# A convolutional attention block on one core: the work beside the attention steps ordered by a small planner

## The chip, the core and the metric

The kernel runs on one core of a Trainium2 chip. Its engines are TensorE (PE, matmul, with PEld as its weight loads), VectorE (DVE), ScalarE (ACT), GpSimd (POOL) and SyncE (SP, which here issues DMAs). Each engine runs its own queue in order; a semaphore holds back an instruction whose data or buffer isn't ready, and with it everything behind it on that engine. The metric is the device time of one execution in microseconds (us).

## The reference

The input x has 8 images of 64 x 64 positions with 256 channels (4096 positions an image), all in float32. Two layers follow each other. Cut to what matters:

```python
# layer 0
q, k = jnp.split(x @ w_qkv + b_qkv, 2, axis=-1);  v = k
ctx_h = _sdpa(h_windows(q), h_windows(k), h_windows(v))   # channels 0..127: 8 windows of 8 rows, 4 heads of 32
ctx_v = _sdpa(v_windows(q), v_windows(k), v_windows(v))   # channels 128..255: 8 windows of 8 columns, 4 heads of 32
hv = hard_swish(v)
bias_branch = depthwise_conv_3x3(hv, dw) + dw_bias
context = hard_swish(concat(ctx_h, ctx_v) + bias_branch)
x = context @ w_out + b_out
# layer 1: spectrally normed weights kf, kg, kh (256 to 32) and kv (32 to 256)
f, g, h = x @ kf + bf, x @ kg + bg, x @ kh + bh
beta = softmax(g @ f.T)                                    # 4096 x 4096 for each image
out = gamma * ((beta @ h) @ kv + bv) + x
```

## The kernel before

Channels lie on partitions, positions along the free axis, in 8 blocks of 512 positions. For each image there are 8 horizontal window units (h0 to h7), 8 vertical ones (v0 to v7) and 8 global ones (l0 to l7, each 512 queries against all 4096 positions). A window unit has 4 steps, a global one 8, so an image has 128 steps and the kernel 1024. The units run in the order h, v, h0 of the next image, l, then h1 and so on.

A step scores(c) is four matmuls (one for each group of 32 partitions) into one set of four PSUM banks (the pool ps_sc has one buffer) and one exponential on ACT over 128 x 2048 values (L281) into a weight buffer p. There are three weight buffers (pool ptp). One step later, weighted(c) multiplies the weights with the values (L467 for windows, L622 for global units) into num. The function run_units walks through all steps: scores of this step, pieces that must come first, the weighted product of the step before, then the pieces that were put at this step.

The sums of the weights, which the softmax divides by, are made in part on DVE and in part on PE. In a window unit, weights 0 and 1 are added on DVE into acc (L476, at step 2, when weighted(1) runs); the sum of acc over keys is a product with ones on PE at step 3, and weights 2 and 3 are summed by two products (L480) at step 0 of the next unit. In a global unit each step adds its weights into acc on DVE (L628, L630); at the end acc is folded (L636, L637) and summed by one product. acc has one buffer for all units. release copies num to SBUF on ACT (L489, L634). norm (L288 to L292 and L494 or L643) transposes the sums, takes their reciprocals, transposes back and multiplies; for vertical units it then sends the result through DRAM (via, shuf) to get back to the row layout (L501, L503 on SP).

The other pieces are:

- project(i, m, k): half a projection of block i, a product of four 512-column matmuls (L68); with k = 1 also the evacuation on ACT (L343 to L362). m = 0 and 2 are queries and keys of the horizontal windows, m = 1 and 3 those of the vertical windows.
- values(kind, i): 16 small matmuls that transpose the keys of a block (pv, L68) and a copy on ACT (L425).
- swish(i, half): hard swish of the keys on DVE (L374, L386) into hv, with halo rows copied by POOL (L393, L394).
- conv(i, half, taps): the depthwise convolution of a block and half of the channels into act. Tap 0 is an activation on ACT (L402), taps 1 to 8 are each one DVE instruction (L406).
- context of a unit: adds the attention to act and applies the hard swish (L517 or L524, L526, L527 on DVE).
- next_layer(i): the projection for layer 1 (pf), an evacuation on ACT (L543), five DMAs on SP, and a transposition of h (ph, L553, L558).
- queries of a global unit: four DMAs on SP (L574); result(m, k): thirds of the output projection (po), an evacuation (L664) and a DMA (L665).

The order of the pieces is written out by hand at the end of attention: spread deals a list of pieces evenly over given steps, finish_window puts release at step 0 and norm at step 1 of the next unit, ahead of what is there, finish_global places norm and the six thirds of the output at fixed steps. Convolutions run in four pieces of two DVE taps (the first with tap 0), one in each step of a unit. A second, exact path repeats the computation where a check of the sums fails; it isn't taken with these inputs.

Of the kernel before, what the change touches and what calls it, by code (L numbers as in the profile page):

```python
# [2 lines left out]

# [12 lines left out]
P = 128  # L16
# [16 lines left out]
class Unit:  # L33
# [4 lines left out]
    def __init__(self, steps, scores, values):  # L38
        self.steps, self.scores, self.values = steps, scores, values
        self.at = [[] for _ in range(steps)]  # L40
        self.first = [[] for _ in range(steps)]


def run_units(units):
    held = None

    def late():
        nonlocal held
        if held is not None:
            held[0].values(held[1])  # L50
        held = None

    for unit in units:
        for c in range(unit.steps):
            unit.scores(c)
            for piece in unit.first[c]:
                piece()
            late()
            for piece in unit.at[c]:
                piece()  # L60
            held = (unit, c)
    late()
# [9 lines left out]
def tile_attention_blocks(  # L72
# [181 lines left out]
    def attention(images, load_x, out_rows, exact):  # L254
# [3 lines left out]
        sfx = "e" if exact else ""  # L258
        state = pools.enter_context(tc.tile_pool(name=f"state{sfx}", bufs=1))
# [5 lines left out]
        ptp = pools.enter_context(tc.tile_pool(name=f"ptp{sfx}", bufs=2 if exact else 3))  # L265
# [32 lines left out]
        def negated_rows(negm, name):  # L298
# [12 lines left out]
            nm = work.tile([P, TB], F32, tag="nm", name=f"nm_{name}", bufs=2)  # L311
# [5 lines left out]
        def image(b):  # L317
            hv, qh, kh, kn, xt, vs, part = {}, {}, {}, {}, {}, {}, {}
            recs = work.tile([P, 3 * NB, TB // D], F32, tag="recs", name=f"recs_{b}")

            def note():
                for t, op in zip(seen, (ALU.max, ALU.min)):
                    nc.vector.tensor_tensor(t, t, recs, op)

# [83 lines left out]
            def conv_pieces(i, half):  # L408
                return [
                    lambda t=t: conv(i, half, t) for t in ((0, 1, 2), (3, 4), (5, 6), (7, 8))  # L410
                ]

# [14 lines left out]
            def window_unit(kind, i):  # L427
# [34 lines left out]
                def weighted(c):  # L462
                    if c == 0:
                        u["num"] = ps_av.tile([P, TB], F32, tag="num", name=f"num_{nm}")
                        u["sum"] = ps_av.tile([P, TB], F32, tag="sum", name=f"sum_{nm}")
# [6 lines left out]
                    if c == 1:  # L472
                        u["acc"] = work.tile(
                            [P, NQ, TB], F32, tag="acc", name=f"acc_{nm}", bufs=1
                        )
                        nc.vector.tensor_add(u["acc"], u.pop(0), u.pop(1))  # L476
# [401 lines left out]
```

## Time and profile before

| what | value |
|---|---|
| timed runs | 4035.29, 4036.5, 4038.03 us; median 4036.5 us |
| profiled execution | 4039.26 us, of it span from first to last instruction 4037.4 us |
| mean granted TensorE clock | 0.980 |
| POOL busy | 163.0 us (4%) |
| x loads on SP | 113 of 512 KB, 3.9 us each from issue to landing |
| chain that ended last | PE 57%, ACT 24%, DVE 12%, issue 3%, DMA 2% |
| costliest group | L281 ACT, global exponentials: 512 x 1.880 us = 962.5 us |
| taps on DVE (L406) | 1024 x 0.749 us = 766.0 us |
| adds of weights on DVE | 384 x 2.292 us (L630), 64 x 2.292 (L628), 2 x 64 x 2.285 (L476) |

A row such as "L476 DVE TENSOR_TENSOR acc_v<-p_v,p_v" names the source line, the engine, the operation and the tiles that are written and read. In the timeline, the first two numbers are start and duration in us; the bracket at the end is the engine's idle time just before, and what ended it. Busy shares are means over stages in which different things are waited for, so that what a piece costs is read from the steps around it.

### The profile page before, as it was taken

Reading aid. Unit: us, or ns where it says so; the run is one execution under the profiler, and the core shown is the slowest. Engines: PE = TensorE matmul, PEld = TensorE weight load, DVE = VectorE, ACT = ScalarE, POOL = GpSimd, SP = SyncE. Lnnn points to the kernel's source line nnn. Section 1 sums busy time; section 2 is a strip of 40 time slices with the busy share of each in tenths; the row PEclk is TensorE's granted clock in tenths of the full one; section 3 lists DMA queues with packets and bytes.
Section 4 is the critical chain, followed back from the end, with each engine's and each line's share of the span. In section 5 each row is a group of like instructions: output and inputs, shape, how many; then the busy total and the mean of one; then the engine's idle time right before and its main releaser. Section 6 shows DMA issues by size and latency. Waiting matters only on the chain.

```text
span 4037.4 us, 74304 instructions
## 1 busy us (share of the span) xinstructions
PE 3638.5 (90%) x32296; PEld 1030.2 (26%) x32296; DVE 2992.6 (74%) x3308; ACT 2530.1 (63%) x2058; POOL 163.0 (4%) x521
## 2 busy tenths in 40 slices
PE   7988998889988899898998899988999889998887
PEld 2222222222222222222222222222222222222221
DVE  4776778767787677876778767787677867777776
ACT  4655766656666666666666666665676656666565
POOL 0000000000000000000000001000010000000000
PEclk9999999999999999999999999999999999999999
DMA  1011110111101111011110111101111011110100
GB/s 39 17 38 43 50 51 17 44 45 44 53 12 44 46 53 43 14 47 43 51 48 12 50 49 43 49 13 52 41 50 43 13 50 44 48 43 19 43 27 30
DMA packets 126335, 157.64 MB, mean 39 GB/s; under 512 B 20528, under 2 KB 62000, under 8 KB 126000
## 3 DMA queue, kind: packets, MB, share of 16 engines
q1 hardware_dynamic: 123312, 152.12, 12.2%
q8 instruction: 255, 4.18, 0.4%
q10 hardware_dynamic: 2688, 0.69, 0.1%
q14 instruction: 80, 0.66, 0.1%
HBM read 77.23 MB, written 50.33 MB: 32 GB/s over the span
## 4 chain that ended last, share of the span: by engine, by line
PE 57%; ACT 24%; DVE 12%; issue 3%; DMA 2%; SPq 1%; ACTq 0%; DVEq 0%
ACT p_l L281 15%; PE s_l L604 15%; PE pq L68 8%; PE s_h L450 7%; ACT p_h L281 5%; PE num_l L622 4%; DVE act L406 4%; PE po_l L68 4%; PE num_h L467 3%; PE sum_h L480 3%; PE s_v L450 3%; PE pv L68 3%; PE sum_v L480 3%; DVE acc_v L476 2%; ACT p_v L281 2%
## 5 line engine op out<-in xcount | busy, mean ns | idle before, releaser
L281 ACT ACTIVATE p_l<-s_l 128x2048 f32<-128x2048 f32 x512 | 962.5, 1880 | 535.7 <-PE s_l L604 503.0
L406 DVE SCALAR_TENSOR_TENSOR act<-hv,dw_sb,act 128x512 f32<-128x512 f32 x1024 | 766.0, 749 | 374.4 <-ACT act L402 350.9
L630 DVE TENSOR_TENSOR acc_l<-acc_l,p_l 128x2048 f32<-128x2048 f32 x384 | 880.1, 2292 | 50.9 <-ACT p_l L281 27.2
L604 PE MATMUL s_l<-g_l,f 32*128 32x512 f32 x4096 | 609.2, 648 | 124.2 <-ACT p_l L281 69.9
L281 ACT ACTIVATE p_v<-s_v 128x2048 f32<-128x2048 f32 x256 | 481.2, 1880 | 354.5 <-DVE acc_v L476 185.4
L281 ACT ACTIVATE p_h<-s_h 128x2048 f32<-128x2048 f32 x256 | 481.4, 1881 | 206.0 <-PE s_h L450 186.8
L622 PE MATMUL num_l<-p_l,h_sb 128*32 128x512 f32 x4096 | 546.3, 605 | 0.1
L68 PE MATMUL pq<-x,wqkv_sb 128*32 128x512 f32 x4096 | 521.0, 601 | 24.4 <-DMA x<-in_xT 15.5
L628 DVE TENSOR_TENSOR acc_l<-p_l,p_l 128x2048 f32<-128x2048 f32 x64 | 146.7, 2292 | 319.7 <-ACT p_l L281 319.7
L450 PE MATMUL s_v<-qv,kv 32*128 32x512 f32 x2048 | 295.9, 648 | 80.7 <-ACT p_v L281 79.3
L450 PE MATMUL s_h<-qh,kh 32*128 32x512 f32 x2048 | 296.6, 649 | 39.7 <-ACT p_h L281 39.7
L604 PEld LDWEIGHTS s_l<-g_l,f 32*128 32x128 f32 x4096 | 173.7, 185 | 582.1 <-ACT p_l L281 485.1
L467 PE MATMUL num_h<-p_h,vs 128*32 128x512 f32 x2048 | 278.8, 617 | 0.0
L467 PE MATMUL num_v<-p_v,vs 128*32 128x512 f32 x2048 | 273.6, 606 | 0.0
L68 PE MATMUL po_l<-act,wout_sb 128*32 128x512 f32 x2048 | 253.9, 593 | 0.0
L393 POOL COPY hv<-hv 128x64 f32<-128x64 f32 x112 | 124.5, 1112 | 3100.6 <-DVE hv L386 3100.6
L68 PEld LDWEIGHTS pq<-x,wqkv_sb 128*32 128x32 f32 x4096 | 134.1, 111 | 336.6 <-issue 303.1
L622 PEld LDWEIGHTS num_l<-p_l,h_sb 128*32 128x32 f32 x4096 | 80.5, 108 | 382.7 <-issue 333.5
L476 DVE TENSOR_TENSOR acc_h<-p_h,p_h 128x2048 f32<-128x2048 f32 x64 | 146.3, 2286 | 10.8 <-ACT p_h L281 10.7
L480 PE MATMUL sum_v<-acc_v,ones 128*32 128x512 f32 x512 | 74.8, 659 | 87.8 <-DVE acc_v L476 87.8
L450 PEld LDWEIGHTS s_v<-qv,kv 32*128 32x128 f32 x2048 | 81.6, 186 | 264.2 <-ACT p_v L281 200.0
L476 DVE TENSOR_TENSOR acc_v<-p_v,p_v 128x2048 f32<-128x2048 f32 x64 | 146.2, 2284 | 0.0
(192 smaller groups left out, 3095.0 us busy)
## 6 DMA issues: line engine op xcount, KB each, us to landing
x<-in_xT SPq DMA_DIRECT2D x113, 512.0 KB, 3.9
out<-ot_l SPq DMA_DIRECT2D x128, 256.0 KB, 2.0
via_v<-nums_v SPq DMA_DIRECT2D x64, 256.0 KB, 2.0
shuf_v<-via_v SPq DMA_DIRECT2D x256, 64.0 KB, 2.0
g_l<-gq SPq DMA_DIRECT2D x256, 64.0 KB, 2.0
f<-fgh SPq DMA_DIRECT2D x256, 16.0 KB, 1.8
gq<-fgh SPq DMA_DIRECT2D x64, 64.0 KB, 2.0
wqkv_sb<-in_w_qkv SPq DMA_DIRECT2D x1, 512.0 KB, 3.8
```

The source lines that it names most:

```text
L68: nc.tensor.matmul(out[quad(r), :], lhsT=lhsT[:, quad(r)], rhs=rhs, start=start, stop=stop)
L281: nc.scalar.activation(pt, sc, AF.Exp, scale=scale)
L393: nc.gpsimd.tensor_copy(before[:, 9, 1 : W + 1], v[:, 1, 1 : W + 1])
L406: nc.vector.scalar_tensor_tensor(o, src, wt, o, ALU.mult, ALU.add)
L450: nc.tensor.matmul(sc[:, r, :], lhsT=k[quad(r), c * P : (c + 1) * P], rhs=q[quad(r), :], start=True, stop=not exact,)
L467: nc.tensor.matmul(u["num"][quad(r), :], lhsT=vs[kind, i][:, c, quad(r)], rhs=u[c][:, r, :], start=(c == 0), stop=(c == 3),)
L476: nc.vector.tensor_add(u["acc"], u.pop(0), u.pop(1))
L480: nc.tensor.matmul(u["sum"][quad(r), :], lhsT=ones[:, :D], rhs=pt[:, r, :], start=(z == "acc"), stop=(z == 3),)
L604: nc.tensor.matmul(sc[:, r, :], lhsT=f4[quad(r), c, :], rhs=u["g"][quad(r), :], start=True, stop=not exact,)
L622: nc.tensor.matmul(u["num"][quad(r), :], lhsT=h_sb[:, c * 4 + r, :], rhs=pt[:, r, :], start=(c == 0), stop=(c == NB - 1),)
L628: nc.vector.tensor_add(u["acc"], u.pop(0), u.pop(1))
L630: nc.vector.tensor_add(u["acc"], u["acc"], u.pop(c))
```

## The change

Nothing that is computed changes; the order in which pieces are put into the engines' queues does. The classes Unit and run_units, and the hand-written places, are taken out. A planner (Flow) walks through the same 1024 steps in the same order. A Task has pieces, a cost, a due step, other tasks that it needs (with a lag in steps) and an earliest step. Two lanes are kept: lane 0 for PE work, lane 1 for DVE work. In each step the fixed pieces of that step come first; then each lane takes the waiting task that is due first, until its budget of 3.25 or 3.3 is used. Costs are constants in the source. What is needed and hasn't been placed is called up at once by require.

The sums of a window unit move: the add of weights 0 and 1 stays at step 2, as a fixed piece; the sum of acc is at step 3, that of weights 2 at step 0 of the next unit, that of weights 3 at its step 1, and norm is at its step 2. In a global unit the sum product stays two steps after the unit's end and norm moves to three steps after it. The projection for layer 1 is split in two pieces. A load of x is issued when the last piece that reads its buffer has been placed, and its own readers wait two steps. The core of the diff, in the lines of the changed kernel:

```diff
-class Unit:
-def run_units(units):
+PROD, ADD, FOLD, NORM, SWISH, TAPS, CONTEXT = 0.86, 2.3, 1.95, 2.5, 1.15, 1.5, 1.9
+class Flow:
+    def require(self, *tasks):
+        for task in tasks:
+            if task.done is not None:
+                continue
+            if task.blockers:
+                self.require(*task.blockers)
+            elif task in self.waiting[0] + self.waiting[1]:
+                self.require(*(n for n, _ in task.needs))
+                while task.done is None:
+                    self.piece(task)
+    def choose(self, lane):
+        if lane == 0 and self.open is not None:
+            return self.open
+        tasks = [k for k in self.waiting[lane] if k.can_start(self.t)]
+        return min(tasks, key=lambda k: k.due) if tasks else None
+    def step(self, scores, values):
+        spent = list(self.base) if scores else [0.0, 0.0]
+        spent[1] += self.behind
+        if scores:
+            scores()
+        for piece in self.first.pop(self.t, ()):
+            piece()
+        if self.held:
+            self.held()
+        self.held = values
+        for piece, lane, cost in self.fixed.pop(self.t, ()):
+            piece()
+            spent[lane] += cost
+        for lane in range(2):
+            goal = self.fill[lane]
+            if lane == 0:
+                goal = max(goal + self.spare, spent[lane] + self.rate())
+            while True:
+                task = self.choose(lane)
+                if task is None or spent[lane] + task.cost / 2 > goal:
+                    break
...
+                spent[lane] += task.cost
+                self.piece(task)
+        self.spare = min(max(self.spare + self.fill[0] - spent[0], -PROD / 2), PROD / 2)
+        self.behind = max(0.0, spent[1] - self.fill[1])
+        self.t += 1
...
-                    if c == 1:
-                        u["acc"] = work.tile(
...
-                        nc.vector.tensor_add(u["acc"], u.pop(0), u.pop(1))
-                    for z in {2: ["acc"], 3: [2, 3]}.get(c, ()):
...
+                def add():
+                    u["acc"] = work.tile([P, NQ, TB], F32, tag="acc", name=f"acc_{nm}", bufs=1)
+                    nc.vector.tensor_add(u["acc"], u.pop(0), u.pop(1))
+                def sums(z):
...
+        flow = Flow(base=(1.95, 0.0), fill=(3.25, 3.3))
...
+        for u in units:
+            e = u.t + u.steps
+            if hasattr(u, "fold"):
+                for c in range(1, NB):
+                    flow.at(u.t + c + 1, partial(u.add, c), 1, ADD)
+                u.released = fixed_piece(e, partial(lambda u: (u.must(), u.release()), u))
+                flow.at(e, u.fold, 1, FOLD)
+                flow.at(e + 2, u.sums, 0, PROD)
+                u.normed = fixed_piece(e + 3, u.norm, 1, NORM)
+            elif hasattr(u, "add"):
+                flow.at(u.t + 2, u.add, 1, ADD)
+                for c, z in ((3, "acc"), (4, 2), (5, 3)):
+                    flow.at(u.t + c, partial(u.sums, z), 0, PROD)
+                u.released = fixed_piece(e, partial(lambda u: (u.must(), u.release()), u))
+                u.normed = fixed_piece(
+                    e + 2, partial(lambda u: (u.must_norm(), u.norm()), u), 1, NORM
+                )
...
+            def conv_task(i, half):
+                needs = [(sw[min(i + 1, NB - 1), half], 2)]
+                if last:
+                    needs += [(k, 0) for k in last.results[i]]
+                due = (h[i].t + 7) if half == 0 else v[i].t + 7
+                taps = ((0, 1, 2), (3, 4), (5, 6), (7, 8))
+                pieces = [partial(im.conv, i, half, k) for k in taps]
+                cv[i, half] = flow.add(1, Task(pieces, TAPS, due, needs))
...
+                    lag = 3 if kind else 1
+                    context[kind, i] = flow.add(
+                        1,
+                        Task(
+                            [u.context], CONTEXT, u.t + (11 if kind else 9),
+                            [(cv[i, kind], 0), (u.normed, lag)],
+                        ),
+                    )
...
+                if i > 1:
+                    h[i].must = lambda i=i, context=context: flow.require(context[0, i - 2])
+                    v[i].must_norm = lambda i=i, context=context: flow.require(context[1, i - 2])
+                    l[i].must = lambda i=i, im=im: flow.require(*im.results[i - 2])
...
-        def spread(unit, pieces, steps):
-        def finish_window(unit, after):
-            after.at[0].insert(0, unit.release)
-            after.at[1].insert(0, unit.norm)
-        def finish_global(unit, after):
...
         with tc.manual_schedule():
-            start()
-            run_units(units)
-            end(units[-1])
+            order_loads()
+            for u in units:
+                for c in range(u.steps):
+                    assert flow.t == u.t + c
+                    flow.step(partial(unit_scores, u, c), partial(unit_values, u, c))
+            flow.drain()
```

The rest of the diff builds the tasks of projections, transpositions, swishes, results and loads in the same way.

## The prediction

> **What bounds the kernel now.** I read the engines' shares first, then the table of waits, then the timeline of two units, then the granted clock in short windows.
>
> ```profile
> PE 3638.5 (90%) x32296; PEld 1030.2 (26%) x32296; DVE 2992.6 (74%) x3308; ACT 2530.1 (63%) x2058; POOL 163.0 (4%) x521
> ```
>
> No engine is full over 4037.4 us, so order decides. The 1024 attention steps follow one another through one set of score banks: scores (PE), exponential (ACT), and only then the next scores. Everything else of a step is queued in between. The timeline of ACT gives the price of a step, from one exponential (L281) to the next.
>
> ```profile
> 1653.66 1.88 ACT L281 ACTIVATE p_h<-s_h 128x2048 f32<-128x2048 f32 x1 [0.54 <-PE s_h L450]
> ...
> 1659.16 1.88 ACT L281 ACTIVATE p_h<-s_h 128x2048 f32<-128x2048 f32 x1 [0.44 <-PE s_h L450]
> ...
> 1720.97 1.88 ACT L281 ACTIVATE p_v<-s_v 128x2048 f32<-128x2048 f32 x1 [0.55 <-PE s_v L450]
> 1722.74 0.58 ACT L489 COPY nums_v<-num_v 128x512 f32<-128x512 f32 x1
> 1723.21 0.82 ACT L402 ACTIVATE act<-hv,dwb_sb,dw_sb 128x512 f32<-128x512 f32 x1
> 1724.75 1.88 ACT L281 ACTIVATE p_v<-s_v 128x2048 f32<-128x2048 f32 x1 [0.72 <-PE s_v L450]
> 1727.95 1.88 ACT L281 ACTIVATE p_v<-s_v 128x2048 f32<-128x2048 f32 x1 [1.32 <-PE s_v L450]
> 1730.59 0.69 ACT L543 ACTIVATE fgh<-pf,bcomb 96x512 f32<-96x512 f32 x1 [0.76 <-PE pf L68]
> 1733.53 1.88 ACT L281 ACTIVATE p_v<-s_v 128x2048 f32<-128x2048 f32 x1 [2.25 <-DVE acc_v L476]
> ```
>
> Call a group of four 512-column matmuls beside the attention (half a projection, a sum of weights, a third of an output) one product; a block's transposition counts as one. The first pair, a step with four products, is 5.50 us. In the unit from 1720.97 the step with two products takes 3.78, the one with none 3.20. So a product costs 0.86 above two, and a step costs 3.20 with up to one, 3.78 with two, 4.64 with three, 5.50 with four. The last step there has two (3.78) and took 5.58: its exponential waited for the add of weights, DVE L476. DVE in the same unit:
>
> ```profile
> 1724.07 1.54 DVE L406 SCALAR_TENSOR_TENSOR act<-hv,dw_sb,act 128x512 f32<-128x512 f32 x2 [3.36 <-ACT act L402]
> 1725.52 0.69 DVE L517 TENSOR_TENSOR tmp_v<-shuf_v,act 128x512 f32<-128x512 f32 x1
> ...
> 1727.31 0.71 DVE L288 STREAM_TRANSPOSE zt_v<-sum_v 128x512 f32<-128x512 f32 x1
> ...
> 1729.70 1.53 DVE L406 SCALAR_TENSOR_TENSOR act<-hv,dw_sb,act 128x512 f32<-128x512 f32 x2
> 1731.15 2.28 DVE L476 TENSOR_TENSOR acc_v<-p_v,p_v 128x2048 f32<-128x2048 f32 x1
> ```
>
> Read it as a queue. The taps start at 1724.07, 3.10 after the unit's first exponential, because tap 0 stands on ACT behind the exponential and the evacuation. Then two taps (0.75 each), a context (start to next start 1.79), the norm (1727.31 to 1729.70: 2.39), two taps, the add; 0.10 after its end the fourth exponential starts. It needs the buffer of weights 0, which the add frees (three buffers). The waits say how much this is:
>
> ```profile
> ACT p_v L281 <- DVE acc_v L476: 185.4, 57, 9.7
> ACT p_h L281 <- DVE acc_h L476: 15.3, 8, 1.9
> DVE act L406 <- ACT act L402: 350.9, 120, 5.7
> ```
>
> **What the old order costs.** The steps of the old order by products: 493 with none or one, 432 with two, 29 with three, 56 with four, 13 with five, one with eight: 1577.6+1633.0+134.6+308.0+82.7+8.9 = 3744.7 us. The first exponential starts at 46.9. So 4037.4-46.9-3744.7 = 245.8 us are lateness beyond these prices: per image 8.4 where the first vertical unit's fourth exponential waits 9.7, some 5.6 and 4.0 around the two borders to and from the global units, 1.65 net in each of five vertical units; the rest is small or the last step's.
>
> **The change, part by part.** Work is conserved: the same matmuls, activations and vector instructions; only seven more loads of x on SP (120 for 113).
>
> *Evener steps.* The new order has 472 steps with none or one, 454 with two, 77 with three, 11 with four, 8 with five, one with seven, one with eight: 1510.4+1716.1+357.3+60.5+50.9+17.0 = 3712.2. Gain 32.5 us. It is no more because below two products a step can't go under 3.20. Ahead of the first exponential stand four products instead of nine: -5 x 0.86 = -4.3.
>
> *Old lateness.* The piles behind it (eight taps, two contexts and a norm ahead of the add in the first vertical unit; queries just ahead of the first global unit) are dissolved. All 245.8 goes out of the sum, and I count the new lateness from nothing, in a steady image.
>
> *The norm moves to the add's step.* With weights 2 and 3 summed in the next unit's steps 0 and 1, the norm goes from step 1 to step 2, fixed pieces in order of units: on DVE it stands directly ahead of the pair's add, which still must end before the fourth exponential. The planner also puts a whole half of a convolution (eight taps) into steps 0 and 1, where before two taps stood in each step. So, from the first exponential:
> - v1: 3.10 + 8 x 0.75 + 2.39 + 2.28 + 0.10 = 13.87; its three steps have 1, 2, 0 products: 3.20+3.78+3.20 = 10.18. Late 3.7.
> - v2, v3: 3.10 + 6 x 0.75 + 1.79 + 2.39 + 2.28 + 0.10 = 14.16 against 1, 2, 2 products, 10.76. Late 3.4 each. v4 to v7 have no taps left: nothing.
> - h3: in step 1 tap 0 stands on ACT behind a query evacuation; 3.8 late, h4 2.3, h5 2.5; each gives back some 0.6, as the following step's PE work is done by then. Net 3.3+1.6+2.0.
> - h0: norm and add behind a copy of h: 1.3.
>
> *A new wait on ACT.* The copy that evacuates a unit's numerators (L489) reuses the buffer of the unit two before, whose context must be done. Where the planner is behind, that context is called up in the same step, behind a half of taps: h6 and v0. In v0: tap 0 ends 2.6 after the exponential before, + 8 x 0.75 + 0.73 (the context's first add) = 9.3; then copy and tap 0 (1.3 net), and behind them on ACT the next exponential: 10.6 against 6.4. Late 4.2. Then 0.15 + 6.0 + 2.39 + 2.28 + 0.10 = 10.9 to the fourth, against 3.78+3.20: 3.9 more. h6 likewise: 4.4 and 3.1, 0.6 back. Together 8.1+6.9.
>
> *Global units.* acc has one buffer, so a unit's first add waits for the sum product of the unit before, in step 2. It starts 1.7 after that step's exponential: 1.7+2.29+0.10 = 4.1 against 3.20, four units x 0.9. In units 3 and 5, keys and a tap 0 lie together on ACT (0.69+0.68+0.82) and four taps ahead of the add in one: 1.6 and 3.1. Unit 7: 0.4. Together 8.7. Bounds for these: nothing (the adds lag within three buffers) and twice.
>
> Sum per image: v1 to v3 10.5, v0 8.1, h6 6.9, h3 to h5 6.9, h0 1.3, global 8.7: 42.4. Eight images: 339.
>
> *Moved DMAs.* The norm's write and four reads, and the loads of x, move on SP; a row of context waits for shuf only 0.7 us in all today, and lag three steps (over 9.6 us) is kept for them. The seven loads take 3.9 each to land and are issued two steps ahead, so 0; without that cover 27 us.
>
> *Clock.* Two windows of the profile: columns are length, busy time of PE, PEld, DVE, ACT, POOL, then the granted clock.
>
> ```profile
> 1566.00:1569.40 3.40, 1.17 (x16) 0.48 (x16) 2.63 (x4) 2.30 (x3) 0.00 (x0) 1.00 0.41 146
> 1569.50:1572.90 3.40, 3.40 (x16) 0.52 (x8) 0.37 (x1) 0.69 (x1) 0.00 (x0) 0.50 0.00 0
> ```
>
> After a stretch with 1.17 us of PE work in 3.40, the next ran at half clock. The late units leave PE idle for 2.1 to 4.5 us, eleven times an image. A sum product at half clock (1.7) still fits under an exponential (1.88); sum and transposition (1.8 to 3.6) don't: 1.7 in each of h3 to h6, say 6 an image, 48 in all. Bounds: 0, and 1.9 in each of eleven, 21 an image. [...]
>
> Last step's lateness as now 13.9; transposition steps 3.86 for 3.78, 16 x 8 x 0.08 = 10.
>
> 4037.4 - 4.3 - 32.5 - 245.8 + 339 + 48 + 13.9 + 10 = 4165.7. The profiled run's own time is 4039.26 and the runs shown lie 0.9 us below the span; I forecast **4165**.
>
> **Rivals.**
> - *Taps not held by tap 0* (faster). If DVE had its taps ready at a unit's start, 3.10 would go in v1 to v3, v0, h6 and about as much again over h3 to h5: 21 an image, and most of the idle gaps: 4165-170-40 = 3955. It decides once new lateness, clock included, is under 32 an image instead of 48. For it: planner lags between swish and convolution. Against: the 350.9 us that DVE waits for tap 0 in 120 cases today. 0.06.
> - *The order isn't what the fill aims at, old lateness stays*: 4037.4-36.8 = 4000. Against: the counts of steps did change. 0.02.
> - *Evacuation copies do not wait* (the contexts come in time): without 4.2 and 4.4, 4100. Against: eight taps can't be done in one step. 0.13.
> - *The clock drops at each gap*: 4165+120 = 4285. For: today each idle stretch over 2.2 us shows it. 0.13.
> - My sum: 0.66.
>
> **Numbers.** The range 4095 to 4260 holds the likeliest case, the case without ACT's wait and part of the clock's. No change that a measurement can tell means within 0.2%, 8 us. Faster 0.08 (first two), same 0.01, slower 0.91.
>
> **What would show it.** Waits of p_v and p_h for the pair's add grow from 200 us to over 250 and spread to the horizontal units; the 9.7 us wait goes; nums copies show waits for DVE; steps with two products stay 3.78; more short stretches at 0.50 clock. Wrong if the fourth exponentials wait under 1 us each, or if the global units change by more than 100 us either way.

## The result and the profile after

The changed kernel takes 4244.39 us (median; 4237.78 to 4245.94), the kernel before 4036.22 in the same comparison. The ratio is 1.0512, with a 95% interval of 1.0494 to 1.053: slower by about 5%, as forecast, and inside the range, but 79 us above the 4165 forecast. The profiled execution took 4237.78 us, its span 4235.9, its mean granted clock was 0.961 (0.980 before).

First the engines' shares of the changed kernel:

```profile
PE 3711.2 (88%) x32296; PEld 1036.5 (24%) x32296; DVE 3020.8 (71%) x3308; ACT 2521.8 (60%) x2058; POOL 112.2 (3%) x521
```

The instruction counts of PE, PEld, DVE, ACT and POOL are those of before: no work was added. PE was busy 73 us longer with the same matmuls, so some ran slower; for the other 126 of the 198 us it stood idle longer. The table of waits (who waits, for whom: us in all, times, longest) says where:

```profile
DVE act L496 <- ACT act L492: 500.7, 127, 10.1
...
ACT p_v L369 <- DVE acc_v L559: 144.1, 36, 5.7
ACT p_h L369 <- DVE acc_h L559: 142.3, 42, 5.3
ACT p_l L369 <- DVE acc_l L719: 130.3, 56, 3.7
DVE acc_l L719 <- PE sum_l L155: 121.9, 28, 6.4
...
ACT nums_h L575 <- DVE tmp_h L610: 75.5, 15, 5.4
```

(L369 is the exponential, L559 and L719 the adds, L492 and L496 the taps, L155 the products, L575 the evacuation.) Before, exponentials of windows waited 185.4 + 15.3 = 200.7 us for the add, nearly all in vertical units, up to 9.7 each. Now it is 286.4, spread evenly over both kinds. Two more stand out: exponentials of global units wait for their first add (130.3, 32.7 before), which itself now waits for the sum product of the unit before, and the evacuation of horizontal units waits for a context, a wait that wasn't there before.

One unit shows the first of these. DVE in v1 of the fourth image (start, us, engine, line, operation, out<-in; the bracket is idle time and who ended it):

```profile
1817.13 6.26 DVE L496 SCALAR_TENSOR_TENSOR act<-hv,dw_sb,act 128x512 f32<-128x512 f32 x8 [5.55 <-ACT act L492]
1823.32 0.71 DVE L376 STREAM_TRANSPOSE zt_v<-sum_v 128x512 f32<-128x512 f32 x1
...
1825.09 0.69 DVE L580 TENSOR_TENSOR nums_v<-nums_v,rr_v 128x512 f32<-128x512 f32 x1
1825.70 2.28 DVE L559 TENSOR_TENSOR acc_v<-p_v,p_v 128x2048 f32<-128x2048 f32 x1
```

and ACT there:

```profile
1814.04 1.88 ACT L369 ACTIVATE p_v<-s_v 128x2048 f32<-128x2048 f32 x1 [2.27 <-PE s_v L535]
...
1821.20 1.88 ACT L369 ACTIVATE p_v<-s_v 128x2048 f32<-128x2048 f32 x1 [0.54 <-PE s_v L535]
1828.08 1.88 ACT L369 ACTIVATE p_v<-s_v 128x2048 f32<-128x2048 f32 x1 [4.99 <-DVE acc_v L559]
```

Eight taps, which began 3.09 us after the unit's first exponential, then the norm, then the add: the fourth exponential starts 14.04 after the first (the prediction added up 13.87), against 10.18 by the prices.

The second, ACT at the start of v0 of the same image:

```profile
1790.99 1.88 ACT L369 ACTIVATE p_v<-s_v 128x2048 f32<-128x2048 f32 x1 [0.62 <-PE s_v L535]
1797.55 0.58 ACT L575 COPY nums_h<-num_h 128x512 f32<-128x512 f32 x1 [4.68 <-DVE tmp_h L610]
1798.03 0.81 ACT L492 ACTIVATE act<-hv,dwb_sb,dw_sb 128x512 f32<-128x512 f32 x1
1798.74 1.87 ACT L369 ACTIVATE p_v<-s_v 128x2048 f32<-128x2048 f32 x1
```

The copy waits 4.68 us, and the next exponential is behind it in ACT's queue, though its scores were long done on PE:

```profile
1792.92 1.14 PE L535 MATMUL s_v<-qv,kv 32*128 32x512 f32 x8 [0.21 <-ACT p_v L369]
```

The third is in the global units. The first add of l1 of the same image, the fourth and fifth exponentials, and the scores between them:

```profile
1977.66 2.29 DVE L719 TENSOR_TENSOR acc_l<-p_l,p_l 128x2048 f32<-128x2048 f32 x1 [6.42 <-PE sum_l L155]
1980.04 1.88 ACT L369 ACTIVATE p_l<-s_l 128x2048 f32<-128x2048 f32 x1 [2.33 <-DVE acc_l L719]
1981.97 2.07 PE L694 MATMUL s_l<-g_l,f 32*128 32x512 f32 x8 [2.07 <-ACT p_l L369]
1984.15 1.88 ACT L369 ACTIVATE p_l<-s_l 128x2048 f32<-128x2048 f32 x1 [2.23 <-PE s_l L694]
```

PE is idle for 2.07 us until that exponential is done, and the next scores take 2.07 us, where the eight of v0 above took 1.14. Windows around this (length, busy time of PE, PEld, DVE, ACT, POOL with counts, then granted clock, DMA share, GB/s):

```profile
1975.20:1978.60 3.40, 3.17 (x32) 0.73 (x24) 0.94 (x1) 2.51 (x3) 0.00 (x0) 1.00 0.81 225
1978.60:1982.00 3.40, 1.33 (x16) 0.19 (x12) 3.30 (x6) 1.88 (x1) 0.50 (x4) 1.00 0.03 6
1982.00:1985.40 3.40, 3.40 (x16) 0.86 (x20) 3.37 (x3) 1.25 (x1) 0.00 (x0) 0.51 0.01 2
```

In the second window the exponential of the fourth step waits for the first add, so PE has only 1.33 us of work; in the third the clock is 0.51, and 16 of PE's instructions take longer than 32 did in the first. Summed over the trace's clock records, PE stood at half clock for 330.9 us in 77 stretches, against 162.6 in 26 before.

By the terms of the prediction (first exponential, steps at their prices, lateness beyond them): 46.9 + 3744.7 + 245.8 before, 42.7 + 3712.2 + 481.0 now. The steps did become cheaper, as counted; the lateness, forecast at 411 with clock and last step, came to 481. By kind of unit, horizontal units went from 1108.7 to 1182.3 us in all, vertical ones from 1077.5 to 1083.1, global ones from 1804.3 to 1927.8: more than half of the loss lies in the global units.

### The profile page after: what moved, and what is told of

It is laid out like the page before. It is cut to its first block, busy times and chain, and to the rows that moved or that the text cites. A ratio compares the mean times of both kernels' runs of the same rounds, so it can differ in the third digit from the quotient of the medians.

```text
span 4235.9 us, 74363 instructions
## 1 busy us (share of the span) xinstructions
PE 3711.2 (88%) x32296; PEld 1036.5 (24%) x32296; DVE 3020.8 (71%) x3308; ACT 2521.8 (60%) x2058; POOL 112.2 (3%) x521
## 4 chain that ended last, share of the span: by engine, by line
PE 54%; DVE 24%; ACT 18%; issue 3%; DMA 0%; ACTq 0%; DVEq 0%; POOL 0%; POOLq 0%
PE s_l L694 12%; DVE act L496 11%; ACT p_l L369 9%; PE pq L155 7%; PE num_l L710 7%; PE po_l L155 6%; PE s_v L535 4%; PE s_h L535 4%; ACT p_v L369 3%; DVE acc_l L719 3%; PE sum_h L566 3%; PE num_v L551 3%; PE num_h L551 2%; ACT p_h L369 2%; DVE acc_h L559 2%
## 5 line engine op out<-in xcount | busy, mean ns | idle before, releaser
L369 ACT ACTIVATE p_l<-s_l 128x2048 f32<-128x2048 f32 x512 | 962.2, 1879 | 624.2 <-PE s_l L694 477.3
L496 DVE SCALAR_TENSOR_TENSOR act<-hv,dw_sb,act 128x512 f32<-128x512 f32 x1024 | 769.3, 751 | 533.1 <-ACT act L492 500.7
L369 ACT ACTIVATE p_v<-s_v 128x2048 f32<-128x2048 f32 x256 | 480.8, 1878 | 337.3 <-PE s_v L535 191.0
L369 ACT ACTIVATE p_h<-s_h 128x2048 f32<-128x2048 f32 x256 | 480.8, 1878 | 275.8 <-DVE acc_h L559 142.3
L710 PE MATMUL num_l<-p_l,h_sb 128*32 128x512 f32 x4096 | 570.0, 630 | 0.1
L155 PE MATMUL pq<-x,wqkv_sb 128*32 128x512 f32 x4096 | 501.2, 599 | 0.1
L535 PE MATMUL s_v<-qv,kv 32*128 32x512 f32 x2048 | 308.3, 673 | 55.0 <-ACT p_v L369 52.8
L551 PE MATMUL num_v<-p_v,vs 128*32 128x512 f32 x2048 | 289.7, 640 | 30.4 <-ACT nums_h L575 28.8
L155 PE MATMUL po_l<-act,wout_sb 128*32 128x512 f32 x2048 | 270.1, 622 | 0.0
L719 DVE TENSOR_TENSOR acc_l<-p_l,p_l 128x2048 f32<-128x2048 f32 x64 | 146.5, 2290 | 172.5 <-PE sum_l L155 121.9
L155 PEld LDWEIGHTS pq<-x,wqkv_sb 128*32 128x32 f32 x4096 | 135.1, 112 | 315.5 <-issue 313.3
L483 POOL COPY hv<-hv 128x64 f32<-128x64 f32 x112 | 66.5, 594 | 3215.2 <-DVE hv L476 3171.5
L559 DVE TENSOR_TENSOR acc_h<-p_h,p_h 128x2048 f32<-128x2048 f32 x64 | 146.3, 2286 | 7.1 <-PE sum_l L155 5.9
L566 PE MATMUL sum_h<-p_h,ones 128*32 128x512 f32 x1024 | 147.0, 648 | 0.0
L559 DVE TENSOR_TENSOR acc_v<-p_v,p_v 128x2048 f32<-128x2048 f32 x64 | 146.2, 2285 | 0.0
```

The costliest lines, as they stand in the source:

```text
L155: nc.tensor.matmul(out[quad(r), :], lhsT=lhsT[:, quad(r)], rhs=rhs, start=start, stop=stop)
L369: nc.scalar.activation(pt, sc, AF.Exp, scale=scale)
L483: nc.gpsimd.tensor_copy(before[:, 9, 1 : W + 1], v[:, 1, 1 : W + 1])
L496: nc.vector.scalar_tensor_tensor(o, src, wt, o, ALU.mult, ALU.add)
L535: nc.tensor.matmul(sc[:, r, :], lhsT=k[quad(r), c * P : (c + 1) * P], rhs=q[quad(r), :], start=True, stop=not exact,)
L551: nc.tensor.matmul(u["num"][quad(r), :], lhsT=vs[kind, i][:, c, quad(r)], rhs=u[c][:, r, :], start=(c == 0), stop=(c == 3),)
```

## The experiments

All times are medians of the comparison. The kernel before was run beside each and took 4031 to 4036 us; ratios are to it, with 95% intervals. Lateness and half-clock time are worked out from each kernel's own trace as above.

| kernel | us | ratio | steps at their prices | lateness | half clock, us (stretches) |
|---|---|---|---|---|---|
| before | 4036.2 | 1 | 3744.7 | 245.8 | 162.6 (26) |
| changed | 4244.4 | 1.0512 (1.0494 to 1.053) | 3712.2 | 481.0 | 330.9 (77) |
| add_first | 4066.8 | 1.0072 (1.0055 to 1.0089) | 3712.2 | 319.0 | 225.0 (53) |
| sums_back | 4040.3 | 1.0012 (0.9999 to 1.0025) | 3717.7 | 273.5 | 218.2 (47) |
| ctxh3 | 4288.5 | 1.0621 (1.0603 to 1.0638) | 3720.5 | 523.5 | 416.1 (91) |
| after_t | 4148.7 | 1.0281 (1.0264 to 1.0299) | 3717.1 | 390.0 | 303.7 (70) |
| lsum1 | 4124.1 | 1.0232 (1.0215 to 1.0249) | 3706.2 | 373.8 | 249.5 (46) |
| warm8 | 4221.1 | 1.046 (1.0442 to 1.0477) | 3712.2 without the added | | 252.9 (52) |
| warml6 | 4234.3 | 1.0496 (1.0479 to 1.0514) | 3712.2 without the added | 482.7 | 286.3 (57) |
| bsums | 4039.4 | 1.0023 (1.0014 to 1.0033) | 3688.7 | 297.6 | 165.4 (19) |
| bbest | 3964.7 | 0.9834 (0.9818 to 0.9851) | 3744.7 | 171.7 | 133.1 (13) |
| sb_l1 | 3922.5 | 0.9727 (0.9711 to 0.9744) | 3711.7 | 167.3 | 75.1 (14) |
| best_fill325 | 3867.1 | 0.9582 (0.9566 to 0.9598) | 3716.0 | 108.5 | 82.3 (11) |
| best | 3798.0 | 0.9412 (0.9396 to 0.9428) | 3693.8 | 63.1 | 38.3 (6) |

### The norm behind the add (add_first)

```diff
         for u in units:
+            if hasattr(u, "add") and not hasattr(u, "fold"):
+                flow.at(u.t + 2, u.add, 1, ADD)
+        for u in units:
             e = u.t + u.steps
...
-                flow.at(u.t + 2, u.add, 1, ADD)
```

The order that the planner fills does not change otherwise; only two neighbours in DVE's queue change places.

> The changed kernel with one edit: in the third step of a window unit the add of weights 0 and 1 is queued on DVE ahead of the norm of the unit before, not behind it; everything else keeps its place. Theory (the norm's 2.39 us ahead of the add is what the fourth exponential waits for): v0 to v3, h3 to h6 and h0 give back up to 2.39 us each, some 19 us an image, 150 us over eight images, and up to 30 more because fewer idle stretches slow the clock: 4060 to 4100 us, and the waits of p_v and p_h for the add fall from 286 us to about 130. Rival (the late norm then holds up the sum product that needs its bank, and the contexts behind it): less than 60 us come back, 4185 us or more, with new waits of PE for DVE's transposition. Second rival (the clock is the main cost): under 30 us come back.

4066.8 us: 178 came back, as expected. DVE in the same unit, v1 of the fourth image:

```profile
1734.82 4.69 DVE L496 SCALAR_TENSOR_TENSOR act<-hv,dw_sb,act 128x512 f32<-128x512 f32 x6
1739.43 2.28 DVE L559 TENSOR_TENSOR acc_v<-p_v,p_v 128x2048 f32<-128x2048 f32 x1
1741.63 0.71 DVE L376 STREAM_TRANSPOSE zt_v<-sum_v 128x512 f32<-128x512 f32 x1
```

and the waits:

```profile
DVE tmp_v L603 <- DMA shuf_v<-via_v: 187.7, 42, 7.1
...
ACT p_v L369 <- DVE acc_v L559: 66.3, 31, 3.9
PEld sum_v L566 <- DVE zt_v L376: 50.4, 28, 3.2
ACT p_h L369 <- DVE acc_h L559: 42.6, 25, 3.0
PEld sum_h L566 <- DVE zt_h L376: 42.5, 28, 3.0
```

The exponentials' wait for the add falls from 286.4 to 108.9 us. The two traced runs differ by 165 us (one was the longest of its four, the other the shortest); by their steps the window units are 172 shorter and the global ones some 10 longer. The rival's waits are there too: PE for the late norm's transposition, and contexts for their loads (73.3 us in the changed kernel). They cost little here: a sum product and a context had slack, the add had none.

### The sums and the norm as before (sums_back)

```diff
-                for c, z in ((3, "acc"), (4, 2), (5, 3)):
+                for c, z in ((3, "acc"), (4, 2), (4, 3)):
...
-                    e + 2, partial(lambda u: (u.must_norm(), u.norm()), u), 1, NORM
+                    e + 1, partial(lambda u: (u.must_norm(), u.norm()), u), 1, NORM
```

> The changed kernel with one part undone: the sum products of weights 2 and 3 go together into the next unit's first step, and the norm into its second, as before the change; the planner fills around them. Theory (norm and eight taps together ahead of the add make the fourth exponential late): with the norm a step earlier the planner puts only two taps beside it and the rest behind the add, so v2, v3 and h5 lose their 3.4, 3.4 and 2.6 us, v1 goes from 3.9 to some 2.2, v0 and h6 have three taps fewer ahead of the waiting copy (2.2 each): about 20 us an image, 4055 to 4090 us. Rival (the planner's piling of taps is enough by itself, wherever the norm stands): within 50 us of the changed kernel, 4195 or more.

4040.3 us, 15 less than the lower end of what was expected, and not to be told from the kernel before. With the norm in the second step the planner places two taps beside it and the others behind the add; v2, v3 and h5 are then on time, the fourth exponential of v1 is 2.2 late instead of 3.8, and the first steps of h6 and v0 0.2 and 0.8 instead of 4.6. h0, h6 and v0 are still 7.3, 2.1 and 4.5 late over their four steps. So the loss is the pair: the norm at the add's step, and a planner that fills the two steps before it with eight taps.

### Three buffers for the copies (ctxh3)

```diff
                     u["num_sb"] = work.tile(
-                        [P, TB], F32, tag="nums" if kind else "ctxh", name=f"nums_{nm}"
+                        [P, TB], F32, tag="nums" if kind else "ctxh", name=f"nums_{nm}",
+                        bufs=2 if kind or exact else 3,
                     )
...
-                    h[i].must = lambda i=i, context=context: flow.require(context[0, i - 2])
+                    if i > 2 or exact:
+                        h[i].must = lambda i=i, context=context: flow.require(
+                            context[0, i - (2 if exact else 3)]
+                        )
```

> The changed kernel with three buffers instead of two for the evacuated numerators of the horizontal units, so that a copy on ACT asks for the context of the unit three before. Theory (the copy's wait on ACT costs 4.4 us in each of h6 and v0): the wait of the nums copies for DVE (75.5 us) goes, and 60 to 70 us come back, 4175 to 4185 us. Rival (the wait only shows that DVE is behind: without it the same work of DVE makes the fourth exponential late a step or two later): within 25 us of the changed kernel, 4220 to 4270 us, with the waits of p_v and p_h for the add grown by about as much as the copy's wait shrank.

4288.5 us: 44 longer than the changed kernel, beyond what even the rival expected. The wait that was taken away is gone from the table, and:

```profile
DVE act L496 <- ACT act L492: 610.2, 128, 10.1
...
ACT p_v L369 <- DVE acc_v L559: 224.5, 49, 7.9
...
ACT p_h L369 <- DVE acc_h L559: 154.0, 41, 5.3
```

The first step of h6 is on time and that of v0 0.3 to 1.6 late (4.6 each before). But the third steps of v0, v1 and v2 are 4.75 late each (2.2, 3.8 and 2.8 on average before), those of v4 to v6 1.5, and h4 and h7 lose 1.5 and 2.9 more there. The reason stands in the order: a context that is called up takes the rest of its convolution with it. Without that call the convolutions slide back; in v0 to v2 tap 0 comes in the second step, behind an exponential and a copy on ACT, and four taps, norm and add only after it, and the last convolutions reach into v4 to v6, which had none. The copy's wait showed that DVE was behind with convolutions; a third buffer alone does not take its cost out. What the wait would cost with the order of the convolutions unchanged, this run does not show.

### Tap 0 as a piece of its own (after_t)

```diff
-                taps = ((0, 1, 2), (3, 4), (5, 6), (7, 8))
+                taps = ((0,), (1, 2), (3, 4), (5, 6), (7, 8))
```

> The changed kernel with tap 0 of a convolution (on ACT) as a piece of its own, so that the planner can place it a step ahead of the taps on DVE and charges it like two of them; the norm stays ahead of the add. Theory (3.10 us of the lateness in v1 to v3, h5, v0 and h6 is DVE standing behind tap 0): v1 to v3 lose 3.8, 3.4 and 3.4, h5 2.6, v0 and h6 2.3 each, 18 us an image: 4080 to 4130 us, and DVE's wait for tap 0 falls from 501 to under 300 us. Rival (the norm and the number of taps ahead of the add are what counts, not when DVE may begin): 4190 us or more.

The edit also raises what the planner counts for a half convolution, from four pieces of 1.5 to five, so that it spreads the taps more; this run does not tell the two effects apart.

4148.7 us, between the two. The waits:

```profile
DVE act L496 <- ACT act L492: 254.8, 83, 9.8
...
ACT nums_h L575 <- DVE tmp_h L610: 118.6, 23, 5.4
```

The vertical units did what was expected: 98 us shorter, v1 to v3 on time within 0.7. The horizontal ones did not get shorter: h3 came on time, but now the copy in h4 waits as well (4.7 late), because the planner placed the same DVE work elsewhere. The global units became 13 longer.

### A global unit's sum product a step earlier (lsum1)

```diff
-                flow.at(e + 2, u.sums, 0, PROD)
+                flow.at(e + 1, u.sums, 0, PROD)
```

> The changed kernel with the sum product of a global unit one step earlier (second instead of third step of the next unit), so that the next unit's first add finds the acc buffer free. Theory (the first add waits for the sum product of the unit before): the 1.03 us late in the third step of l1, l2, l4 and l6 goes, 33 us over eight images, and with it the steps at half clock that follow it (l1, l2, l4, l6, fourth and fifth step, some 40 us): 4170 to 4215 us; the wait of the add for the sum product (121.9 us of DVE) goes. Rival (the lateness in the steps after it has nothing to do with the wait): 33 us or less come back, 4210 us or more, with half-clock time still near 330 us.

4124.1 us: 120 came back (113 by the ratios) where 30 to 74 were expected. The wait of the first add for the sum product is gone, the lateness of the global units falls from 139 to 41 us. Of these 98 us, 50 are the fourth and fifth steps of l1 to l6, for some 40 expected, and 48 the steps ahead of them, for 33: l5, whose third step was 2.4 late by four taps and the same wait together, is on time there as well. Beyond that the order of the window units came out otherwise: 41 us less lateness in vertical units, 32 more in horizontal ones, and 6 us less in steps at their prices.

### Work for an idle PE (warm8, warml6)

```diff
                     if z == "acc":
                         u["sum"] = ps_av.tile([P, TB], F32, tag="sum", name=f"sum_{nm}")
+                        if not exact and i in ((0, 1, 2, 3) if kind else (3, 4, 5, 6)):
+                            for k in range(8):
+                                nc.tensor.matmul(
+                                    u["sum"][quad(k % NQ), :], lhsT=ones[:, :D],
+                                    rhs=wqkv_sb[:, 0, :], start=True, stop=True,
+                                )
                     pt = u.pop(z)
```

> The changed kernel with eight additional 512-column matmuls (1.7 us at full clock) in the fourth step of h3 to h6 and v0 to v3, just ahead of the sum product that waits for the add; they write the sum bank, which the sum product then starts anew, so the result is the same. They run where PE stands idle waiting for the add. Theory of the clock (idle stretches in these units halve the clock afterwards and that costs more than the 48 us predicted): half-clock time falls from 331 us to under 230 and 40 to 100 us come back, 4145 to 4205 us. Rival (the half clock falls where nothing waits for PE): half-clock time falls, the time stays within 20 us of 4244. Second rival (the additional matmuls are not hidden): up to 110 us longer.

4221.1 us: 23 came back with 78 us less at half clock, 0.3 us for each. That is under what the theory expected (40 or more, half-clock time under 230) and just over the rival's 20: the half clock costs time, but in these units most of it lies where nothing waits for PE. The changed kernel's own trace shows such a place. In v0 the second step is 1.1 to 2.4 us late from one image to another, with the half clock, but second and third step together are 4.16 or 4.17 late in each of the later seven images: the queue on DVE sets the fourth exponential, and what PE loses ahead of it adds nothing.

For the global units:

```diff
                     product(nc, u["sum"], ones, u["acc"][:, 0, :])
+                    if not exact:
+                        spare = mm_tile(f"spare_{nm}")
+                        for k in range(6):
+                            nc.tensor.matmul(
+                                spare[quad(k % NQ), :], lhsT=ones[:, :D],
+                                rhs=wqkv_sb[:, 0, :], start=True, stop=True,
+                            )
```

> The changed kernel with six additional 512-column matmuls (1.3 us at full clock) behind each global unit's sum product, into a spare bank that nothing reads. The wait of the next unit's first add (1.03 us) stays. Theory (the steps after that wait are late because the idle PE is then granted half the clock): half-clock time falls by 60 us or more, the 45 us late in the fourth and fifth steps of l1 to l6 go, 4185 to 4215 us. Rival (those steps are late for another reason, and the additional matmuls lie on the path): 4235 us or more.

4234.3 us: by the time alone the rival, since it is not to be told from the changed kernel; half-clock time fell by 45 us, not 60. The trace says more. The same place of l1 as above:

```profile
1973.10:1976.50 3.40, 3.09 (x24) 0.58 (x18) 3.37 (x4) 1.24 (x1) 0.50 (x4) 1.00 0.12 32
1976.50:1979.90 3.40, 2.71 (x24) 0.86 (x28) 3.30 (x5) 2.08 (x2) 0.00 (x0) 1.00 0.02 7
```

Here the second window, in which the add is waited for, holds additional matmuls (24 instructions for 16), the next one is granted 1.00 and its exponential comes on time. In the changed kernel the fourth and fifth steps of l1 to l6 are 49.8 us late in all; here 7.1 are left, nearly all in l5's fifth. The wait ahead of these steps is still there, so that lateness is the clock's. The additional matmuls took the gain back: 0.3 us in the third steps, 1.2 in l7 and 1.7 in the h1 that follows, where PE isn't idle.

### One part of the change in the old order (bsums)

In the kernel before, with its order by hand (and contexts of vertical units one step later):

```diff
         def finish_window(unit, after):
-            after.at[0].insert(0, unit.release)
-            after.at[1].insert(0, unit.norm)
+            after.at[0][:0] = [lambda: unit.sums(2), unit.release]
+            after.at[1].insert(0, lambda: unit.sums(3))
+            after.first[2].insert(0, unit.norm)
...
```

> The kernel before, its hand-written order kept, with one part of the change alone: weights 2 and 3 are summed in the next unit's first and second step, the norm goes to the third step ahead of the add, and contexts of vertical units one step later so that their loads keep their lead. Theory (the norm ahead of the add is dear only together with the eight taps that the planner piles into the first two steps; with two taps a step the same work stands ahead of the add as before): within 30 us of the kernel before, 4005 to 4065 us. Rival (the norm's place costs by itself, up to 2.4 us in each of 16 units an image): 4100 us or more.

4039.4 us, as expected (9 more than the kernel before beside it, at 4030.7), but by two effects that cancel. The steps at their prices come to 56 us less, since one product goes from a unit's first step to its second. Next to none of it shows: lateness grows by 52, of it 34 by 0.7 us in the third step of v1 to v6 of each image. In these units the add's end sets the fourth exponential, and cheaper steps ahead of it only wait longer for it.

### Two better orders

The kernel before with the norm behind the add (contexts of vertical units one step later, not shown) and the pile at the first vertical unit dissolved:

```diff
-            after.at[1].insert(0, unit.norm)
+            after.at[2].insert(0, unit.norm)
...
                 units.append(nxt["h"][0])
+                spread(units[-1], im["conv"](NB - 1, 0), range(4))
+                units[-1].at[3].append(h[-1].context)
                 finish_window(v[-1], units[-1])
...
-                    spread(unit, im["conv"](NB - 1, 0), range(2))
-                    unit.at[3].append(h[-1].context)
+                    if not nxt:
+                        spread(unit, im["conv"](NB - 1, 0), range(2))
+                        unit.at[3].append(h[-1].context)
```

> The kernel before, its hand-written order kept, with the norm in the third step behind the add (contexts one step later), and the last horizontal unit's convolution spread over the next image's first unit instead of piled into the first vertical unit. Theory (DVE work ahead of the add is what the kernel before pays for as well): the 1.65 us of five vertical units and the 8.4 us of the first one go, up to 125 us over the images: 3910 to 3970 us. Rival (the norm behind the add holds the sum bank or the contexts' loads come late): 4010 us or more.

3964.7 us, at the slow end of what was expected: vertical units 108 us shorter, horizontal ones 31 longer, because the convolution now makes the end of h0 late (5.1 to 10.6 in its fourth step).

And the changed kernel with sums_back and lsum1 together:

> Both edits: the sum products of weights 2 and 3 together and the norm a step earlier (4040 us alone), and the sum product of a global unit a step earlier. If the two costs lie in different units and add up: 4040 less 35 to 70, 3970 to 4005 us, below the kernel before (4036). Rival (the wait for the sum product hid something else in the global units, such as the norm's read of the sum bank): 4020 us or more.

3922.5 us, 48 under what was expected, since lsum1 alone gave more than expected. 4040.3 - 120.3 is 3920: the two costs add up. By the ratios too: 0.050 and 0.028 alone, 0.0785 together.

With tap 0 as a piece of its own as well, and the planner's fill for PE lower:

```diff
-        flow = Flow(base=(1.95, 0.0), fill=(3.25, 3.3))
+        flow = Flow(base=(1.95, 0.0), fill=(2.9, 3.3))
```

> The changed kernel with what the runs have shown to be dear taken out: sum products of weights 2 and 3 together and the norm a step earlier, a global unit's sum product a step earlier (3922 us with these two), tap 0 as a piece of its own, and the planner's fill for PE 2.9 instead of 3.25. Steps by products: 572 with none or one, 328 with two, 80 with three, 40 with four, 4 with more, 3694 us at the prices of the prediction; first exponential at 42; lateness from 167 to some 60 to 110. If the piles of taps are what was left: 3790 to 3850 us. Rival (the lateness left is not the taps'): 3890 us or more.

> The last version with the planner's fill for PE put back from 2.9 to 3.25, all else as there, so that it stands between 3922 us (without tap 0 as a piece of its own) and 3798 us. At the prices of the prediction its steps come to 3716 us, 22 more than with 2.9. Theory (the piece of its own dissolves the piles behind tap 0 and is most of the difference): lateness 70 to 110 us, 3830 to 3870 us. Rival (the lower fill, with fewer steps of two products, is what shortens it): 3890 us or more.

3798.0 us, 5.9% faster than the kernel before, and 3867.1 with the fill put back: both lie within what was expected. But tap 0 is not most of the difference: it is worth 55 of the 124 us from 3922, the fill 69. Of the fill's 69 the prices make 22; another 47 are lateness that goes in the unit h0 (54 to 7 us over the images). Engines and waits of the fastest:

```profile
PE 3587.2 (94%) x32296; PEld 1017.1 (27%) x32296; DVE 3018.3 (79%) x3308; ACT 2513.7 (66%) x2058; POOL 112.1 (3%) x521
```

```profile
DVE act L496 <- ACT act L492: 98.8, 60, 5.9
...
ACT nums_h L575 <- DVE tmp_h L610: 36.1, 22, 1.8
ACT p_h L369 <- DVE acc_h L559: 26.4, 15, 2.1
ACT p_v L369 <- DVE acc_v L559: 19.2, 7, 2.7
```

The same instructions; exponentials of windows wait 45.6 us for the add instead of 286.4, and those of global units no longer for theirs.

## Why the prediction was right, and where it was short

*Steps and start.* First exponential 42.7 and 3712.2 us of steps, as counted. Since both are made from the order, this only says that the prices held: in v1 of add_first, with nothing late, the first two steps took 3.20 and 3.79, for 3.20 and 3.78.

*The norm at the add's step.* Shown. The fourth exponentials of v1, v2 and v3 are 3.8, 3.4 and 3.4 late (3.7, 3.4, 3.4 forecast), those of h3 to h5 4.2, 2.5 and 2.6 (3.8, 2.3, 2.5); with norm and add exchanged 178 us came back. That it takes the piled taps too is shown by sums_back and bsums.

*The copy on ACT.* Its size was right (4.6 in each of h6 and v0, for 4.4 and 4.2). As a cost that stands alone it fell: with a third buffer the wait goes and the kernel is longer. The rival that put the kernel without these waits at 4100 counted on a saving that this way of removing them didn't bring.

*Taps behind tap 0.* The rival said that about 21 us an image stand behind tap 0, 170 in all; taking half of that wait away (500.7 to 254.8) gave 96 (88 in the traces: 98 in the vertical units and 1 in the horizontal ones, where the work turned up in other units, and 13 lost in the global ones).

*Global units.* The waits and queues listed in the prediction came to 73 us for 70. But its test ("wrong if the global units change by more than 100") went against it: they grew by 123.5, of it 5.0 by prices.

*Clock.* This is the step that failed, in place and so in size. The prediction counted drops only behind the late window units, eleven an image, and put them at 48 us; in the global units it put nothing. There 49.8 us are measured, in the fourth and fifth steps of l1 to l6, right behind the waits for the add, and warml6 shows the clock to be the cause. The row that the prediction shows (1.17 us of work in a window of 3.40, then a clock of 0.50) tells nothing of the kind of unit, but it was applied to the window units alone. In these the total came out as forecast: an image's window units are 40.3 us late on average over the later seven images, for 33.7 of waits and queues, 6 of clock and 1.3 of transpositions. How much of that is the clock's is not shown; warm8 got 23 us back from eight images. It is not where the prediction put it: of h3 to h6, which were to lose 1.7 each, h4 to h6 are 11.5 late for 10.5 without any clock. And in v0 and h6 a late second step is no cost of its own (second and third step together: 4.2 and 3.3 in each of the later images, 3.9 and 3.1 forecast from DVE's queue).

*All images alike.* The first image's order differs: v4 to v7 and h7 there have a pile each, 4.4 to 5.2 late, while h3, h6 and v0 are less late than in the others. Its window units are 59.7 us late for 41.

So the 70 between 411 and 481 are 57 in the global units (126.3 without the last step, for 69.6) and 19 in the first image, less some 5 in the other window units and 1 in the last step. The remaining 9 of the 79 us lie outside the trace: the profiled run was the shortest of its four, 6.6 under their median, and 1.9 above its span. The time stayed inside the range because the range had room for part of the clock's rival; the sum itself had nothing for the clock in the global units.

*Old lateness.* One reading was off without harm: the net lateness of five vertical units before is 1.2 us each (1.8 in the third step, 0.6 made up in the next), not 1.65. The sum takes the 245.8 out whole.

*The signs named beforehand.* The waits for the pair's add passed 250 us and spread to the horizontal units, the wait of 9.7 went (5.7 is the longest), the copies wait for DVE, steps with two products stay at 3.78, and stretches at half clock are more. The time came to lie between the likeliest case and the rival in which the clock drops at each gap (4285), which is where the clock term belongs.

*DMA.* Forecast at nothing. Contexts waited 73.3 us for shuf (0.7 before), a wait that none of the runs shows to be on the path; with the norm later still (add_first) it was 187.7, and the time shorter.

## What to carry to other kernels

Where one engine's result frees a buffer that the next step needs, put that instruction first in its queue whenever its inputs are ready; here what stood ahead of it was paid (178 us for the norm), and what stood behind it cost little. A planner that fills steps by cost must know the order inside a step and not the sums alone: with the same instructions and the same cost constants, two changes of place, a piece split in two and one setting moved this kernel from 5.1% slower to 5.9% faster. And a wait in a profile isn't yet a cost: it is when taking it away makes the kernel shorter, which the largest new waits here did in two cases (norm, sum product) and not in the third (copy, where the third buffer also changed the order).

## What the runs showed of the hardware

In l1 of the fourth image the changed kernel's PE stood idle for 2.07 us ahead of the half clock, in a window of 3.40 us with 1.33 us of work, and the window behind it was granted 0.51. With six more matmuls ahead of that place (warml6), the two windows shown hold 3.09 and 2.71 us of work, and the clock stayed at 1.00.

In the traces of the kernel before and of the changed one, the 26 and 77 stretches at half clock begin whole multiples of 3.4135 us apart, to within 0.11 us. Cut into windows of that length from these starts, the two traces show the following. Of the windows at full clock (the first 50 us left out), all 86 with less than 1.4 us of PE work were followed by half clock (25 before, 61 in the changed kernel); of those with 1.4 to 1.7 us 15 were and 17 were not; of those with 1.7 us or more 2 were and 2130 were not. What is special about the 2 is open. Across the table, though not row by row, half-clock time falls from 416 to 38 us as lateness falls from 524 to 63: in these runs, where waits were taken away, time at half clock mostly fell with them.
